# A graph-transformer kernel: attention folded in ahead of the last feed-forward's output, experts ranked by logits, and the expert tiles' rows, tables and transposes rearranged

## The chip, the cores and the metric

The kernel runs on one core of one Trainium2 chip. Five engines work in parallel, each with its own in-order queue: PE (TensorE, matrix products and transposes; PEld is its weight load), DVE (VectorE), ACT (ScalarE), POOL (GpSimd) and SP (SyncE). SP issues most transfers and holds a few registers; POOL issues the indirect gathers and scatters. They meet at semaphores. The metric is the device time of one execution in microseconds (us); lower is better.

## The reference, cut to what matters

A node table `x` of 3125 rows by 256 goes through two layers. The first adds, to the input, graph attention over 50,000 edges and a four-layer mixer (linear attention and a feed-forward each); then a mixture of eight experts, two for each node, adds its output. The second layer has another aggregation, another mixer and a dense mixture; nothing of it changes here.

```python
xn = _layernorm(x, axis=-1)
x = x + _L0_gnn_ref(xn, edge_index, ...) + _L0_mix_ref(xn[None], ...)[0]
x = x + _L0_ffn_ref(_layernorm(x, axis=-1)[None], ...)[0]
...
def _L0_ffn_ref(x, gate_w, gate_b, W1, b1, W2, b2):
    logits = xf @ gate_w + gate_b
    probs = jax.nn.softmax(logits, axis=-1)
    top2_vals, top2_idx = jax.lax.top_k(probs, 2)
    cw = jnp.zeros((N, Ee)).at[jnp.arange(N)[:, None], top2_idx].add(top2_vals)
    def step(acc, params):
        w1, bb1, w2, bb2, we = params
        h = jax.nn.gelu(xf @ w1 + bb1, approximate=False)
        y = h @ w2 + bb2
        return (acc + we[:, None] * y, None)
```

All of it is in 32-bit floats. The kernel computes for each node only the two experts with the largest weights, which is the same sum.

## The kernel before, in words

The 3125 nodes are 25 tiles of 128 rows (`NT`; the last has 53). `X`, with all of them, stays in SBUF from start to end.

**The first layer** is one Python loop over the generator `mixer()`. Each `yield` is a turn. In a turn the loop may also take steps of `edges()` (the graph attention, `todo`) and of the first generator in the list `late`. Such side work is put under `queued()` (L303), which says that it is to be issued after the last instruction so far of DVE, ACT and PE; the builder then fixes one order for each engine, and it may place an instruction among those of its neighbours. SP and POOL are not bound by `queued()`.

In the last mixer layer the feed-forward runs over the groups of `LATE`: first three tiles (22 to 24), then five groups of four, then two tiles. The text here calls the last two of these groups 5 and 6. For each group eight products with `w1` (L280 `mm`, hidden features `f`), each followed by a Gelu on ACT (L688), fill `gT`; then for each tile of the group a product with `w2` (L280 `acc`) is added to `X` by DVE (L699). Each product is a turn and each tile is a turn. After a group, `late.append(dispatch(t0, n))` (L706) hands it to the side work.

**`dispatch`** does, for the tiles of one group:
- loads the input rows `x0` (L250) and the attention's sums `ac` (L772), and adds both to `X` with the scale of the running maximum (L775 to L789);
- takes a layer norm (L260 to L264, with a square root on ACT) and normalises the rows into `hd` (L268);
- transposes `hd` on PE (L274), copies on ACT to `hx` (L802), and multiplies by the gate weights (`seg<-wt,hx`): logits `lg` (L806);
- softmax (L316 to L323, an Exp on ACT), rank of each expert among the eight probabilities (L812 to L821, `over`, `took`), weights `cw` (L823);
- transposes `cw` (L329), multiplies by the experts' output biases (L335) and adds to `X` (L336);
- counts on PE how many earlier rows took each expert (L831, L832), from which DVE forms the row `slot` of each token in its expert's stretch of the table `tok` (L836 to L846), and the weights `gate` (L848 to L850);
- POOL writes each row of `hd` to `tok` twice (L854, one indirect transfer per tile and choice).

After the loop whatever is left in `late` is run to its end. Then DVE builds tables (L881 to L932): how many 256-row tiles each expert needs, and for each of the `MT` = 32 tiles its expert `exI`, its first row in `tok` `rowI`, and its biases `b1`; and `slot` is corrected for the padding between experts.

**The expert tiles** (L943 on). For each of 32 tiles SP reads `exI` and `rowI` into registers, and loads two weight blocks (512 KB each) and the 256 rows `hr` (256 KB); three buffers each. PE transposes the rows (L956), DVE copies them to `hTe` (L958), PE makes four products of 128 hidden features (`mm<-hTe,ew`), each with a Gelu on ACT (L963), then the two output products (`acc<-ew,egT`); DVE copies the result to `yo` (L968) and ACT's queue stores it to `yex` (L969). From tile 8 on, every third tile also loads one expert of the second layer's weights (L973). After the loop the second layer gathers from `yex` by `slot`.

The memory of the expert stage's pool is memory that the first layer's pools have released, and the release counts all uses of those pools.

Of the kernel before, what the change touches and what calls it, by code (L numbers as in the profile page):

```python
# [8 lines left out]
F32 = mybir.dt.float32  # L9
# [10 lines left out]
L = 4  # L20
# [167 lines left out]
def fast_path(ctx: ExitStack, tc: tile.TileContext, i, out, ident, dstP):  # L188
# [171 lines left out]
    with ExitStack() as l0:  # L360
# [169 lines left out]
        def mixer():  # L530
# [5 lines left out]
            for l in range(L):  # L536
# [144 lines left out]
                for c, (t0, n) in enumerate(chunks):  # L681
                    nxt = chunks[c + 1][1] if c + 1 < len(chunks) else 0
                    gT = big.tile([Q, NF, n * Q], F32, name="gT", tag="kv", bufs=2)
                    for f in range(NF):
                        pm = ps("mm", [Q, n * Q])
                        product(pm, [w1[:, k, f * 128:(f + 1) * 128] for k in range(KC)],
                                [hT[:, k, t0:t0 + n, :].rearrange("p j c -> p (j c)") for k in range(KC)])
                        nc.scalar.activation(gT[:, f, :], pm, AF.Gelu, bias=col("b1", l * NF + f))  # L688
                        if f % 2 and f // 2 < nxt:
                            ff.rows(c + 1, f // 2)  # L690
                        yield 0.45 * n / NT / NF
# [72 lines left out]
        def dispatch(t0, n):  # L764
# [26 lines left out]

            mv, rs = ln_stats(xs, n)
# [12 lines left out]
            pr = g0.tile([Q, 4, NE], F32, name="lg", tag="lg", bufs=2)[:, 0:n, :]  # L805
            nc.vector.tensor_tensor(pr, pg, bc(gb, 1, n), ALU.add)  # L806
            softmax_of(g0, pr)
            yield
# [3 lines left out]
            nc.vector.tensor_tensor(over, bc(pr, 2, NE), bc(pr, 3, NE), ALU.is_equal)  # L812
            of = over.rearrange("p t e f -> p t (e f)")
            nc.vector.tensor_tensor(of, of, bc(below.rearrange("p e f -> p (e f)"), 1, n), ALU.mult)
            nc.vector.tensor_tensor(more, bc(pr, 2, NE), bc(pr, 3, NE), ALU.is_gt)
            nc.vector.tensor_tensor(over, over, more, ALU.add)
            def small(name):
                return g0.tile([Q, 4, NE], F32, name=name, tag=name, bufs=2)[:, 0:n, :]
# [3 lines left out]
            cw = small("cw")  # L822
            nc.vector.tensor_tensor(cw, took, pr, ALU.mult)  # L823
            yield
            yield from add_biases(g0, t0, n, cw, bt, tag="gt", bufs=3)
# [21 lines left out]
            for k in range(2):  # L847
                nc.vector.tensor_tensor(sel, at, bc(sf[:, k, :], 2, NE), ALU.is_equal)  # L848
                nc.vector.tensor_tensor(sel, sel, cw, ALU.mult)
                nc.vector.tensor_reduce(gate[:, k, t0:t0 + n], sel, AX.X, ALU.add)  # L850
            for j in range(n):
                r = rows(t0 + j)
                for k in range(2):
# [4 lines left out]
                    tc.declare_no_dep(put.ins, group="tok", reason="no two tokens have the same row of an expert")  # L858

# [4 lines left out]
        for step in mixer():  # L864
# [4 lines left out]
            if late:  # L869
                with queued():  # L870
                    if next(late[0], 0) == 0:
                        late.pop(0)
# [6 lines left out]


        tiles = g0.tile([Q, NE], F32, name="tiles", tag="tiles")  # L881
        nc.vector.tensor_tensor(tiles, used, first, ALU.subtract)
        nc.vector.tensor_scalar(tiles, tiles, float(ME - 1), None, op0=ALU.add)
        ti = g0.tile([Q, NE], I32, name="ti", tag="ti")
        nc.vector.tensor_copy(ti, tiles)
        nc.vector.tensor_scalar(ti, ti, 8, None, op0=ALU.logical_shift_right)
        nc.vector.tensor_copy(tiles, ti)
        upto = g0.tile([Q, NE], F32, name="upto", tag="upto")
        nc.vector.tensor_copy(upto, tiles)
        for e in range(1, NE):  # L890
            nc.vector.tensor_tensor(upto[:, e:e + 1], upto[:, e - 1:e], upto[:, e:e + 1], ALU.add)
        nth = g0.tile([Q, MT], F32, name="nth", tag="nth")
        nc.gpsimd.iota(nth, pattern=[[1, MT]], base=0, channel_multiplier=0, allow_small_or_imprecise_dtypes=True)
        eoh = g0.tile([Q, MT, NE], F32, name="eoh", tag="gt", bufs=3)
        nc.vector.tensor_tensor(eoh, bc(upto, 1, MT), bc(nth, 2, NE), ALU.is_le)
        ex = g0.tile([Q, MT], F32, name="ex", tag="ex")
        nc.vector.tensor_reduce(ex, eoh, AX.X, ALU.add)
        nc.vector.tensor_scalar(ex, ex, float(NE - 1), None, op0=ALU.min)
        exI = const.tile([Q, MT], I32, name="exI", tag="exI")
        nc.vector.tensor_copy(exI, ex)  # L900
        eidx = g0.tile([Q, NE], F32, name="eidx", tag="eidx")
        nc.gpsimd.iota(eidx, pattern=[[1, NE]], base=0, channel_multiplier=0, allow_small_or_imprecise_dtypes=True)
        nc.vector.tensor_tensor(eoh, bc(eidx, 1, MT), bc(ex, 2, NE), ALU.is_equal)

        nc.vector.tensor_tensor(tiles, upto, tiles, ALU.subtract)
        nc.vector.scalar_tensor_tensor(tiles, tiles, -float(ME), first, op0=ALU.mult, op1=ALU.add)
        pick = g0.tile([Q, MT, NE], F32, name="pick", tag="gt", bufs=3)
        nc.vector.tensor_tensor(pick, eoh, bc(tiles, 1, MT), ALU.mult)
        row = g0.tile([Q, MT], F32, name="row", tag="row")
        nc.vector.tensor_reduce(row, pick, AX.X, ALU.add)  # L910
        nc.vector.scalar_tensor_tensor(row, nth, float(ME), row, op0=ALU.mult, op1=ALU.add)
        nc.vector.tensor_scalar(row, row, float(NE * ST - ME), None, op0=ALU.min)
        rowI = const.tile([Q, MT], I32, name="rowI", tag="rowI")
        nc.vector.tensor_copy(rowI, row)
        b1 = const.tile([Q, MT, HB], F32, name="b1", tag="b1")
        be = cols_of("e_b1").rearrange("p (e f) -> p f e", f=HB)
        for f in range(HB):
            nc.vector.tensor_tensor(pick, eoh, bc(be[:, f, :], 1, MT), ALU.mult)
            nc.vector.tensor_reduce(b1[:, :, f], pick, AX.X, ALU.add)


        step = g0.tile([Q, NE], F32, name="step", tag="step")
        nc.vector.tensor_copy(step, tiles)
        nc.vector.tensor_tensor(step[:, 1:NE], tiles[:, 1:NE], tiles[:, 0:NE - 1], ALU.subtract)
        sp = g0.tile([Q, 2 * NT, NE], F32, name="sp", tag="gt", bufs=3)
        sl = slotF.rearrange("p k t -> p (k t)")
        nc.vector.tensor_tensor(sp, bc(sl, 2, NE), bc(first, 1, 2 * NT), ALU.is_ge)
        nc.vector.tensor_tensor(sp, sp, bc(step, 1, 2 * NT), ALU.mult)
        back = g0.tile([Q, 2 * NT], F32, name="back", tag="back")
        nc.vector.tensor_reduce(back, sp, AX.X, ALU.add)  # L930
        nc.vector.tensor_tensor(back, sl, back, ALU.subtract)
        nc.vector.tensor_copy(slot.rearrange("p k t -> p (k t)"), back)  # L932

# [6 lines left out]
    with ExitStack() as l0e:  # L940
# [3 lines left out]
        for k in range(MT):  # L944
            re = nc.values_load(exI[0:1, k:k + 1], engines=(SPE,), min_val=0, max_val=NE - 1)
            rr = nc.values_load(rowI[0:1, k:k + 1], engines=(SPE,), min_val=0, max_val=NE * ST - ME)
            w1 = ew.tile([Q, KC, EH], F32, name="ew1", tag="ew1", bufs=3)
            nc.sync.dma_start(w1, i["e_W1"][bass.ds(re, 1), :, :].rearrange("o (k p) c -> p (o k) c", p=Q))
# [1044 lines left out]
```

## Time and profile before

| what | us |
|---|---|
| median of 3 runs (2812.88 to 2814.0) | 2813.36 |
| the profiled execution | 2967.99 |
| its span | 2966.2 |
| PE busy (89% of the span) | 2640.8 |
| DVE busy (51%) | 1517.6 |
| ACT busy (29%) | 873.5 |
| POOL busy (31%) | 917.0 |
| share of the chain that ended last on PE | 79% |

The profile is one execution under the hardware profiler, which is longer than the runs without it. Its page gives busy times, the span in slices, the chain of work that ended last, and groups of instructions. The trace behind it answers questions about a stretch, an engine or a tile: a line of a timeline has the start, the duration, engine, line of the kernel, operation, output and inputs, shape and count, and in brackets the idle time before it with what ended it. A matrix product of 32-bit floats appears as two PE instructions, so `x16` is eight products. In the tile names, numbers of buffers are left out: `ew` is either weight block of an expert, `w` either block of the feed-forward. The mean granted PE clock of the profiled execution is 0.945 of full speed.

### The profile page before, as it was taken

The numbers are of one execution on the slowest core, as the hardware profiler recorded it, in microseconds if no ns is written. First come the engines' busy times: TensorE is split into PE (matmuls) and PEld (weight loads), VectorE is DVE, ScalarE is ACT, GpSimd is POOL, SyncE is SP. The second block draws the span as 40 slices with busy tenths as digits, with TensorE's granted clock in tenths as the row PEclk, the third lists the DMA queues.
The fourth block names the chain that finished last, engine by engine and source line by source line (L and its number), as shares of the span: only waits on it lengthen the run. The fifth ranks groups of instructions, "written<-read, shape, count | busy, mean of one in ns | idle before, by whom it ended". The sixth has DMA issues, their size and how long they took to land.

```text
span 2966.2 us, 29959 instructions
## 1 busy us (share of the span) xinstructions
PE 2640.8 (89%) x10578; PEld 1891.9 (64%) x10578; DVE 1517.6 (51%) x3749; ACT 873.5 (29%) x1621; POOL 917.0 (31%) x964
## 2 busy tenths in 40 slices
PE   5899989989988779898998699856789999999998
PEld 4666768656676457686665588734556666666655
DVE  6376655856657557668556311176834333322211
ACT  3432225312252112343333122222233222322223
POOL 2107542144521335200122100065354544555200
PEclk9899999999999889999998799978889999999999
DMA  4002221022212121100111576442122222222100
GB/s 141 12 16 89 81 90 38 22 77 76 86 47 70 29 77 41 59 4 13 31 58 59 191 252 200 153 145 81 47 75 64 75 67 71 71 73 78 33 8 10
DMA packets 152337, 215.85 MB, mean 73 GB/s; under 512 B 21032, under 2 KB 120686, under 8 KB 152178
## 3 DMA queue, kind: packets, MB, share of 16 engines
q1 hardware_dynamic: 104274, 112.31, 11.7%
q0 software_dynamic: 36848, 91.34, 10.8%
q10 hardware_dynamic: 11056, 10.19, 1.1%
q8 instruction: 86, 1.41, 0.2%
q14 instruction: 73, 0.60, 0.1%
HBM read 160.14 MB, written 53.61 MB: 72 GB/s over the span
## 4 chain that ended last, share of the span: by engine, by line
PE 79%; DVE 10%; another core or an unknown queue 4%; issue 3%; ACT 2%; DMA 1%; POOL 0%; SPq 0%; DVEq 0%; ACTq 0%
PE mm L280 33%; PE acc L280 24%; PE seg L467 6%; PE seg L1241 6%; PE acc L614 3%; PE tr L274 3%; PE seg L280 1%; PE acc L335 1%; DVE vals L457 1%; DVE gt L422 1%; DVE st L521 1%; DMA raw<-in_src 0%; PE tr L280 0%; DVE hT L737 0%
## 5 line engine op out<-in xcount | busy, mean ns | idle before, releaser
L283 POOL DMA_INDIRECT gt<-table,srcI x391 | 426.9, 1092 | 807.1 <-DVE m L425 602.9
L283 POOL DMA_INDIRECT gt<-xtab,srcI x391 | 381.7, 976 | 394.8 <-PE seg L1241 241.9
L280 PE MATMUL mm<-hT,w 128*128 128x512 f32 (+2 forms) x896 | 381.7, 562 | 23.7 <-ACT gT L688 16.2
L280 PE MATMUL acc<-w,gT 128*128 128x256 f32 x1600 | 370.0, 387 | 6.2 <-issue 4.2
L280 PEld LDWEIGHTS acc<-w,gT 128*128 128x128 f32 x1600 | 306.4, 194 | 53.1 <-issue 6.9
L1182 ACT ACTIVATE fh<-mm,bn_b,bn_s 128x512 f32<-128x512 f32 (+1 forms) x224 | 163.1, 731 | 425.8 <-PE mm L280 391.9
L280 PEld LDWEIGHTS mm<-hT,w 128*128 128x128 f32 x896 | 164.5, 193 | 158.8 <-issue 100.0
L339 DVE SCALAR_TENSOR_TENSOR X<-acc,rw,X 128x256 f32<-128x256 f32 x200 | 95.1, 483 | 325.9 <-PE acc L280 277.2
L688 ACT ACTIVATE gT<-mm,cols 128x512 f32<-128x512 f32 (+2 forms) x224 | 142.3, 641 | 354.0 <-PE mm L280 263.5
L280 PE MATMUL mm<-wqkv,hT 128*128 128x256 f32 x800 | 214.2, 399 | 15.6 <-ACT hT L723 9.0
L467 PE MATMUL seg<-vals,oh 128*128 128x261 f32 x782 | 192.0, 399 | 13.3 <-DVE oh L290 8.7
L280 PE MATMUL acc<-fw_f_Wo,fh 128*128 128x256 f32 x800 | 198.4, 385 | 1.6 <-issue 0.7
L280 PE MATMUL mm<-fh,fw_f_W 128*128 128x512 f32 (+1 forms) x448 | 195.3, 565 | 1.6 <-ACT fh L1182 1.3
L1241 PE MATMUL seg<-gt,oh 128*128 128x256 f32 x782 | 186.6, 388 | 3.8 <-DVE sum L1258 2.7
L280 PE MATMUL mm<-xc,fw_f_W 128*128 128x512 f32 (+1 forms) x448 | 188.9, 551 | 0.0
L467 PEld LDWEIGHTS seg<-vals,oh 128*128 128x128 f32 x782 | 152.9, 198 | 52.8 <-DVE oh L290 15.7
L280 PEld LDWEIGHTS acc<-fw_f_Wo,fh 128*128 128x128 f32 x800 | 144.7, 190 | 59.1 <-issue 27.9
L1241 PEld LDWEIGHTS seg<-gt,oh 128*128 128x128 f32 x782 | 150.4, 194 | 38.5 <-issue 12.8
L280 PEld LDWEIGHTS mm<-wqkv,hT 128*128 128x128 f32 x800 | 144.2, 197 | 40.4 <-ACT K L566 11.4
L699 DVE TENSOR_TENSOR X<-acc,X 128x256 f32<-128x256 f32 x100 | 42.2, 422 | 220.8 <-PE acc L280 149.2
L1020 POOL DMA_INDIRECT ye<-yex,slot x50 | 51.5, 1030 | 297.4 <-DVE cb L1087 273.8
L280 PEld LDWEIGHTS mm<-fh,fw_f_W 128*128 128x128 f32 x448 | 78.2, 191 | 99.5 <-issue 68.7
(329 smaller groups left out, 3877.0 us busy)
## 6 DMA issues: line engine op xcount, KB each, us to landing
ew<-in_e_W SPq DMA_DIRECT2D x64, 512.0 KB
tok<-zero SPq DMA_DIRECT2D x8, 3328.0 KB
w<-in_W SPq DMA_DIRECT2D x8, 1024.0 KB
hr<-tok SPq DMA_DIRECT2D x32, 256.0 KB
yex<-yo ACTq DMA_DIRECT2D x32, 256.0 KB
gt<-table,srcI POOLq DMA_INDIRECT x391
gt<-xtab,srcI POOLq DMA_INDIRECT x391
fw_f_W<-in_f_W SPq DMA_DIRECT2D x16, 256.0 KB
```

The lines of the kernel that those rows point to most:

```text
L274: nc.tensor.transpose(pt[:, k, :], src_row[:, k * Q:(k + 1) * Q], ident)
L280: nc.tensor.matmul(pm, a, b, start=(k == 0), stop=(k == len(lhs) - 1))
L283: nc.gpsimd.indirect_dma_start(out=dst, out_offset=None, in_=tab[:, :], in_offset=bass.IndirectOffsetOnAxis(ap=srcI[:, b:b + 1], axis=0))
L335: nc.tensor.matmul(py, cT[:, j, :], bt, start=True, stop=True)
L339: nc.vector.scalar_tensor_tensor(X[:, t, :], py, cw, X[:, t, :], op0=ALU.mult, op1=ALU.add)
L467: nc.tensor.matmul(open_seg[w_], oh[:, b - h0, :], v[:, b - h0, :], start=(b == a), stop=(b == z))
L614: nc.tensor.matmul(cx[a], K[0:r, t, a * 128:(a + 1) * 128], keys.hn[0:r, t, :], start=(t == 0), stop=(t == NT - 1))
L688: nc.scalar.activation(gT[:, f, :], pm, AF.Gelu, bias=col("b1", l * NF + f))
L699: nc.vector.tensor_tensor(X[:, t, :], py, X[:, t, :], ALU.add)
L1020: nc.gpsimd.indirect_dma_start(out=ye[0:r, j, :], out_offset=None, in_=yex[:, :], in_offset=bass.IndirectOffsetOnAxis(ap=slot[0:r, k, t0 + ...
L1182: nc.scalar.activation(hn[:, a, 0:w], pm, AF.Relu, bias=bn[s][1][:, c:c + 1], scale=bn[s][0][:, c:c + 1])
L1241: nc.tensor.matmul(segs[w], oh[:, j, :], gt[:, j, :], start=(b == z), stop=(b == a))
```

## The change

`dispatch` is cut in two. Its first part, the attention and the input rows, becomes `fold`, which is put at the head of `late` at the start of each group of the last feed-forward, so that it is added to `X` before the group's output is. While more than one generator waits in `late`, two steps are taken in a turn.

In `dispatch` the rank is taken from the logits, before any softmax, which gives the same two experts. Counts, slots and the writes to `tok` follow at once; softmax, `cw`, the gate weights and the biases come after.

The first eight tiles of the expert stage are the first tile of each expert: their expert, row and bias are constants. `table_of_tiles` builds the tables for the other 24 (`MR`), in two parts that are taken after tiles 0 and 1; its correction of `slot` compares with two thresholds for each expert. A function `load` issues a tile's transfers, the rows ahead of the weights; three tiles are loaded ahead of the loop, and tile k+3 at the end of tile k. `turned` transposes a tile's rows, and tile k+1's are transposed in tile k, between its two products.

```diff
                     gT = big.tile([Q, NF, n * Q], F32, name="gT", tag="kv", bufs=2)
+                    if l == L - 1:
+                        late.insert(0, fold(t0, n))
...
-        def dispatch(t0, n):
+        def fold(t0, n):
...
             nc.vector.tensor_tensor(x4, x4, a4[:, :, :, 0:64], ALU.add)
             yield
 
+        def dispatch(t0, n):
+
+            xs = X[:, t0:t0 + n, :]
             mv, rs = ln_stats(xs, n)
...
-            nc.vector.tensor_tensor(pr, pg, bc(gb, 1, n), ALU.add)
-            softmax_of(g0, pr)
-            yield
+            lg = small("lg")
+            nc.vector.tensor_tensor(lg, pg, bc(gb, 1, n), ALU.add)
...
-            nc.vector.tensor_tensor(more, bc(pr, 2, NE), bc(pr, 3, NE), ALU.is_gt)
+            nc.vector.tensor_tensor(more, bc(lg, 2, NE), bc(lg, 3, NE), ALU.is_gt)
...
-            cw = small("cw")
-            nc.vector.tensor_tensor(cw, took, pr, ALU.mult)
             yield
-            yield from add_biases(g0, t0, n, cw, bt, tag="gt", bufs=3)
...
-            for k in range(2):
-                nc.vector.tensor_tensor(sel, at, bc(sf[:, k, :], 2, NE), ALU.is_equal)
-                nc.vector.tensor_tensor(sel, sel, cw, ALU.mult)
-                nc.vector.tensor_reduce(gate[:, k, t0:t0 + n], sel, AX.X, ALU.add)
             for j in range(n):
                 r = rows(t0 + j)
                 for k in range(2):
...
+            yield
+
+            softmax_of(g0, lg)
+            cw = small("cw")
+            nc.vector.tensor_tensor(cw, took, lg, ALU.mult)
+            for k in range(2):
+                nc.vector.tensor_tensor(sel, at, bc(sf[:, k, :], 2, NE), ALU.is_equal)
+                nc.vector.tensor_tensor(sel, sel, cw, ALU.mult)
+                nc.vector.tensor_reduce(gate[:, k, t0:t0 + n], sel, AX.X, ALU.add)
+            yield
+            yield from add_biases(g0, t0, n, cw, bt, tag="gt", bufs=3)
...
             if late:
-                with queued():
-                    if next(late[0], 0) == 0:
-                        late.pop(0)
+                for _ in range(2 if len(late) > 1 else 1):
+                    with queued():
+                        if late and next(late[0], 0) == 0:
+                            late.pop(0)
...
-        for k in range(MT):
-            re = nc.values_load(exI[0:1, k:k + 1], engines=(SPE,), min_val=0, max_val=NE - 1)
-            rr = nc.values_load(rowI[0:1, k:k + 1], engines=(SPE,), min_val=0, max_val=NE * ST - ME)
...
+        def load(k):
+            if k < NE:
+                v1, v2, rr = i["e_W1"][k:k + 1, :, :], i["e_W2"][k:k + 1, :, :], k * ST
+                src = tok[rr:rr + ME, :]
+            else:
+                re = nc.values_load(exI[0:1, k - NE:k - NE + 1], engines=(SPE,), min_val=0, max_val=NE - 1)
+                rr = nc.values_load(rowI[0:1, k - NE:k - NE + 1], engines=(SPE,), min_val=0, max_val=NE * ST - ME)
...
+            hr = ew.tile([Q, 2, D], F32, name="hr", tag="hr", bufs=3)
+            nc.sync.dma_start(hr, src.rearrange("(j p) c -> p j c", p=Q))
             w1 = ew.tile([Q, KC, EH], F32, name="ew1", tag="ew1", bufs=3)
...
+        loaded = {k: load(k) for k in range(3)}
+        hT = turned(loaded[0][2])
+        table = table_of_tiles()
+        for k in range(MT):
+            w1, w2, _ = loaded.pop(k)
...
+            if k + 1 < MT:
+                hT = turned(loaded[k + 1][2])
             py = ps("acc", [Q, 2, D])
...
             nc.scalar.dma_start(yex[k * ME:(k + 1) * ME, :].rearrange("(j p) c -> p j c", p=Q), yo)
+            next(table, None)
+            if k + 3 < MT:
+                loaded[k + 3] = load(k + 3)
```

The new `table_of_tiles` has some 45 DVE operations, as many as the block that it replaces; its last part is

```diff
+            sp = tmp("sp", [2 * NT, 2 * NE])
+            sl = slotF.rearrange("p k t -> p (k t)")
+            nc.vector.tensor_tensor(sp, bc(sl, 2, 2 * NE), bc(thr.rearrange("p e s -> p (e s)"), 1, 2 * NT), ALU.is_ge)
+            nc.vector.tensor_tensor(sp, sp, bc(inc, 1, 2 * NT), ALU.mult)
+            back = tmp("back", [2 * NT])
+            nc.vector.tensor_reduce(back, sp, AX.X, ALU.add)
```

## The prediction

> **What bounds the kernel now.** I read the chain of waits first, then busy time by stretch, then the waits inside one stretch. TensorE (PE) carries 79% of the chain that ended last, so only stretches where PE idles or runs slowed are worth anything. The change touches two stretches: from the last mixer layer's feed-forward to the first expert tile, and the 32 expert tiles. The view of busy time by stretch (us in the stretch, busy PE, PEld, DVE, ACT, POOL; clock; DMA share; GB/s):
>
> ```profile
> 1500.00:1550.00 50.00, 48.91 (x214) 35.63 (x213) 26.83 (x100) 14.94 (x22) 14.25 (x15) 1.00 0.19 64
> 1550.00:1600.00 50.00, 46.76 (x206) 32.23 (x205) 25.09 (x95) 22.34 (x34) 8.47 (x8) 1.00 0.17 54
> 1600.00:1620.00 20.00, 14.36 (x60) 11.69 (x58) 12.62 (x53) 3.79 (x8) 4.88 (x6) 0.79 0.12 40
> 1620.00:1650.00 30.00, 12.57 (x38) 7.99 (x38) 22.18 (x107) 3.33 (x6) 14.88 (x15) 0.50 0.22 75
> 1650.00:1665.00 15.00, 0.67 (x4) 0.70 (x4) 5.52 (x16) 0.00 (x0) 0.35 (x1) 0.50 0.43 144
> 1700.00:1800.00 100.00, 94.96 (x454) 81.16 (x455) 16.12 (x26) 24.66 (x52) 0.00 (x0) 1.00 0.74 241
> ```
>
> The feed-forward is PE-bound (48.9 and 46.8 of 50 us busy). Then PE nearly stops for some 55 us. In the tile loop it is busy for 95 of 100 us. The PE timeline and the chain give the gap's ends:
>
> ```profile
> 1600.86 8.86 PE L280 MATMUL acc<-w,gT 128*128 128x256 f32 x32
> 1613.72 0.82 PE L274 MATMUL tr<-ident,hd 128*128 128x128 f32 x4 [4.00 <-DVE gate L850]
> 1634.32 1.09 PE L274 MATMUL tr<-ident,hd 128*128 128x128 f32 x4 [4.91 <-DVE hd L268]
> 1664.33 1.08 PE L956 MATMUL tr<-ident,hr 128*128 128x128 f32 x4 [18.79 <-DMA hr<-tok]
> ...
> 1658.93 4.73 DMA hr<-tok
> 1663.67 0.66 issue
> 1664.33 1.10 PE tr L956 x4
> 1665.45 0.70 DVE hTe L958
> 1666.20 3.70 PE mm L280 x8
> ```
>
> The last output row ends at 1600.86+8.86 = 1609.72; the first expert product starts at 1666.20: 56.5 us. [...] The stations between: slots of group 4 and group 5's normalised rows to 1613.72 (4.0); its gate products to 1618.59 (4.9); its softmax and ranks to 1622.46 (3.9); its counts, slots and biases, with group 6's attention, to 1632.02 (9.6); group 6 from statistics to slots to 1645.51 (13.5); writes, tile tables and SP's register reads to the first load at 1657.74 (12.2); loads, transposes and copy to 1666.20 (8.5). Inside the loop the waits between 1680 and 1920 us (total, times, longest) are:
>
> ```profile
> PEld mm L280 <- DVE hTe L958: 16.0, 15, 1.1
> PE mm L280 <- DVE hTe L958: 12.4, 15, 0.8
> PEld mm L280 <- ACT egT L963: 3.2, 16, 0.4
> ```
>
> Every second tile PE stands about 1.07 us until the transposed rows are copied.
>
> **Transposes a tile ahead.** The built instruction order puts tile k+1's four transposes among tile k's up-products and its copy (0.69 us) beside the down-product (3.46 us). A pair of tiles takes 15.82 us (1684.30 to 1700.12), of which the stall is 1.07 and the rest work that stays. Sixteen pairs: 17 us less, about 7.38 us a tile. What is late next? The loads: the stretch 1700 to 1750 us moves 275 GB/s at share 0.85; the faster pace asks 275x7.91/7.38 = 295 GB/s, share 0.91. Rows of 10 us reach 302 GB/s at 0.88, and 353 in the first burst, and loads have two tiles (15 us) of lead. I count no loss; the upper bound is the whole 17 us. Moving each row load ahead of its weights helps the transposes; a row load and two weight loads cost SP three issues of 0.37 us as before.
>
> **Tile tables and registers.** Before, the tables (DVE, 1643.73 to 1655.66) and 13 reads of 0.42 us on SP (to 1657.74) stand ahead of the first load. After, the first eight tiles have constant rows; 48 reads remain of 64 and fall in the loop, where SP waits for buffers anyway. The tables' some 45 small DVE operations (10 us, and 1.5 more for the slot correction of doubled width) lie beside the first row load and tile 0. If that cover failed, tile 1's copy would be late: some 14 of them (5 us) stand between the copies of tiles 0 and 1, and tile 0 takes 9. Cost nothing.
>
> **But the loads cannot start early.** In the built order SP's first row load waits, because its buffers reuse released memory, for all row writes, the last Exp, the last bias product and the last gate reduction; the weights queue behind it. So softmax, gates and biases are moved behind the writes in the text, yet are still waited for. They fit in DVE's gaps while POOL, which has nothing else here, writes; they cost no more than their places in the queues.
>
> **The drain, counted from the last row's end.** DVE (one addition, the logits of group 5, 13 more operations at the start-to-start intervals seen at 1620, 0.1 to 0.45 us) has group 6's normalised rows ready at 4.5. PE holds ahead of them group 5's counts (1.05) and the transposes of its weights `cw` (1.04), which need the softmax: DVE reaches `cw` at 7.2, so group 6's transposes start at 8.4. With the gate products and four bias products between them they end at 13.0 (alone, before, 1634.32 to 1637.38). Ranks to 16.0, counts 1.05, slots (2.7 us before, plus two bias additions) to 20.7. POOL: group 5's eight writes start at 10.0 and take 8x1.27 = 10.2, up to 11 us; the four of group 6 follow from 20.9 to 26.0. Landing: no row shows it alone; a 256 KB store lands in 2.13, a gather in 6.16; I take 2.1 as a write is nearer a store: 28.1, and SP issues at 28.4. The row load is now first: between 2.13 and the 4.73 seen with 1 MB ahead; I take 2.9, then 1.10 and 0.75 for transposes and copy: 33.2. The first weights (0.77 MB at 353 GB/s and 2.1) land about then. **33.3 us in place of 56.5: 23 saved**; bounds 12 (slow landings, DVE 4 us later) and 28.
>
> Here the Trainium skill speaks against the change: its page "ScalarE: Activation LUTs", section "What ACT_TABLE_LOAD costs", prices each change of table at 2.66 us, load and drain. The Exp table now stands between group 6's square root and group 5's weights. The row:
>
> ```profile
> 1592.11 1.28 ACT L318 ACT_TABLE_LOAD   x1
> 1593.40 0.23 ACT L318 ACTIVATE lg<-lg 128x32 f32<-128x32 f32 x1
> ```
>
> Exp starts 0.01 us after a load of 1.28, with no drain. By the row Exp is done at 4.4, well ahead of DVE's turn; by the page at 5.8, which costs `cw` at most 0.3. The number of loads does not change. I take the row. The Trainium skill's page "TensorE: Matmul & The Clock Gate", Part 1 on the HAM clock gate, has the clock halved until about 3.4 us of sustained work. One might hope that the shorter drain spares the cold start. The first eight PE instructions of expert products take 3.70 us, later eights 1.73: 2.0 us. The idle left (33 us) is still far over that window, so by rule and row those 2.0 us stay, and drain products keep the slow rows' price; a hope of 2 us more is dropped.
>
> **Attention ahead of the output.** `fold` is the same work, moved ahead by one group: DVE's six operations of up to 1.23 us and two loads a group. Both loads pass to before the group's products on SP's queue; SP does nothing else there but edge-table stores, which still come first for the first group. The built order has each load's buffers free long before use; in the first group the table (issued 1400.32) is needed near 1404, a wait DVE can afford as PE has three output rows of 3.46 us queued. Two steps a turn crowd DVE (25 to 27 of 50 us busy) no further on average, but one 1.22 us addition ahead of an evacuation can hold PE. Bounds: 4 us gained (all idle of 1500 to 1600) to 8.5 lost (1.22 for each of 7 groups); I take 2 lost, as idle now is under a microsecond per place. Group 5's gate products now stand ahead of the last row's final products: 2 us of work and as much waiting for copies less overlap, 3 us (0 to 5).
>
> **Sum.** -17 -23 +2 +3 = -35 us on the profiled execution of 2967.99 us (span 2966.2 and 1.8 around it). The median of the runs is 2813.36, 0.948 of it; I scale: -33. **2780 us.** Everything before the last layer's feed-forward and after the loop keeps its order.
>
> **Rivals.**
> - *Loads bind the loop* (15%). For: share 0.9 in several rows at 10 us, and the last experts' weights share the queue. Against: 0.6 after 1760. The loop gains 5: -23, so 2791.
> - *The drain hardly shortens* (13%), since the first load waits for everything: only tables, registers and load order go: the last write ends at 1650.35, with landing 1652.8 instead of 1657.74, and 3.6 on the load: -8.6. With the loop -25: 2789. Against: group 6's attention (over 3 us) and its softmax leave that chain for certain.
> - *Drain overlaps better* (8%), no harm to the feed-forward: -45, 2771.
> - *Slower* (4%). DVE stands in its queue for a fold's table load, with X additions and hT behind it, so PE stops. Price: a wait beyond 3.46 us of cover for each of seven groups; from 5 us exposed per group it decides, at 6 it is 42 lost: 2820. For: the fold computes one turn after its loads, not two. Against: buffers are free early in the built order, and DVE had no such wait at 1602.
> - The likeliest, as summed: 60%.
>
> **Range and chances.** The likeliest's own bounds, combined, give 2768 to 2793; the second and first rival reach 2791, the fourth 2771; to leave out no more than 2 in 10 I take 2766 to 2798. The three runs lie within 0.04%, and 0.2% (5.6 us) is about what a measurement of this kernel can tell from no change: faster by more 0.93, within 0.03 (a small stall of the slower kind), slower 0.04.
>
> **What would show it.** Waits of PE on the copied rows gone and about 7.4 us a tile; no register reads ahead of the first load; some 33 us between last output row and first expert product, with POOL's writes ending about 26 after it; PE idle between 1400 and 1600 about as now. Wrong if PE waits for DVE on rows of the fold, if tiles wait for weights, or if the gap stays over 45 us.

## The result, and the profile after

The changed kernel takes 2773.47 us (median of four runs, 2770.17 to 2777.46) where the kernel before takes 2813.45 (four runs, 2812.88 to 2814.0): a ratio of 0.9864, 95% interval 0.9847 to 0.9881, 40 us less. The forecast was 2780, 33 less. The profiled execution of the changed kernel took 2773.55 us (span 2771.8), as its runs do; so it is not the profiler that made the first profile of before longer than its runs.

The first profile of the kernel before, on which the forecast was built, spans 2966.2 us, 194 more than that of the changed kernel. Most of this is not the change, so a second profile of the kernel before was taken; it spans 2805.8. The table cuts each profile at the same instructions: the start of the last linear-attention product (`acc<-hn,K`), the first product of the last layer's feed-forward, the end of its last output product, the first expert product, the end of the last down-product, the first transpose of `xn` behind the loop, and the end of the span. All stages are differences of start times that the trace gives; where a stage ends with a product, its 0.38 us is added.

| us | before, first profile | before, second | after |
|---|---|---|---|
| start to the last linear-attention product | 1319.9 | 1209.8 | 1209.9 |
| to the feed-forward | 70.8 | 69.6 | 69.6 |
| last feed-forward | 218.9 | 218.9 | 221.3 |
| drain (last output row to first expert product) | 56.5 | 57.1 | 34.6 |
| 32 expert tiles | 254.3 | 254.3 | 238.2 |
| loop's end to `xn` | 21.9 | 21.9 | 21.9 |
| from there to the end | 1023.9 | 974.2 | 976.3 |

Between the two profiles of before, 160 us of difference lie in the first and the last row, and almost nothing in the stages that the change touches. Against the second profile the change brings 2.4 - 22.5 - 16.1 = -36.2 us in its three stages, and the spans differ by 34.0.

Busy time by stretch of the changed kernel (us in the stretch, busy PE, PEld, DVE, ACT, POOL; granted clock; DMA share; GB/s): the end of the feed-forward, cut where PE falls idle and where the clock changes, the drain, and 200 us of the tile loop.

```profile
1481.33:1483.38 2.05, 0.00 (x0) 0.00 (x0) 0.72 (x4) 2.02 (x3) 1.45 (x2) 1.00 0.31 110
1483.38:1493.62 10.24, 9.30 (x23) 6.18 (x24) 5.08 (x19) 2.49 (x4) 4.29 (x5) 0.50 0.19 68
1493.62:1500.86 7.24, 7.24 (x46) 6.17 (x44) 2.33 (x8) 1.29 (x4) 0.00 (x0) 1.00 0.01 2
...
1500.00:1520.00 20.00, 12.20 (x42) 8.08 (x41) 11.48 (x60) 2.77 (x6) 7.78 (x8) 0.60 0.13 48
1520.00:1535.00 15.00, 3.26 (x9) 1.87 (x8) 7.15 (x38) 0.00 (x0) 3.84 (x4) 0.50 0.38 122
```

```profile
1550.00:1750.00 200.00, 200.00 (x981) 174.83 (x980) 37.96 (x55) 51.40 (x109) 0.00 (x0) 1.00 0.77 247
```

In the loop PE is now busy for all of 200 us at full clock: no wait is left there to remove. The drain has shrunk but still has PE idle and at half clock. And inside the feed-forward PE falls idle at 1481.33, and from 1483.38 on the clock is at half for 10.24 us. The kernel before has a stall of another form at the same place; it is taken up below.

PE's timeline of the changed kernel across the drain (start, us, operation, count, and in brackets the idle time before it and what ended it):

```profile
1499.75 1.11 PE L280 MATMUL acc<-w,gT 128*128 128x256 f32 x4
1500.69 0.51 PE L280 MATMUL seg<-wt,hx 128*128 128x8 f32 x4
1504.29 0.64 PE L831 MATMUL seg<-took,earlier 128*128 128x32 f32 x2 [3.09 <-DVE took L824]
...
1507.66 0.64 PE L274 MATMUL tr<-ident,hd 128*128 128x128 f32 x2
...
1514.58 1.22 PE L335 MATMUL acc<-bt,cwT 8*128 8x256 f32 x2
1518.15 0.60 PE L831 MATMUL seg<-took,earlier 128*128 128x16 f32 x2 [2.35 <-DVE sm_r L322]
...
1533.63 1.08 PE L982 MATMUL tr<-ident,hr 128*128 128x128 f32 x4 [10.95 <-DVE upto L917]
1535.50 3.78 PE L280 MATMUL mm<-hTe,ew 128*128 128x256 f32 x8 [0.78 <-DVE hTe L984]
```

The last output row ends at 1500.86 and the first expert product starts at 1535.50. Group 5's gate products (`seg<-wt,hx`) now stand among the last row's products. Group 6's transposes start 6.8 us after the row. The last wait is put down to DVE's `upto`, which these transposes do not read. It is the row load that ends it: when the rows are issued behind the weights (below), the same transposes start 4.3 us later, and in the kernel with both edits (below) the view names `hr<-tok` itself.

### The profile page after: what moved, and what is told of

It is laid out like the page before. It is cut to its first block, busy times and chain, and to the rows that moved or that the text cites. A ratio compares the mean times of both kernels' runs of the same rounds, so it can differ in the third digit from the quotient of the medians.

```text
span 2771.8 us, 29883 instructions
## 1 busy us (share of the span) xinstructions
PE 2596.2 (94%) x10578; PEld 1875.5 (68%) x10578; DVE 1523.5 (55%) x3754; ACT 870.6 (31%) x1619; POOL 932.1 (34%) x962
## 4 chain that ended last, share of the span: by engine, by line
PE 83%; DVE 10%; ACT 2%; DMA 2%; issue 2%; POOL 1%; SPq 0%; DVEq 0%; ACTq 0%; POOLq 0%
PE mm L280 35%; PE acc L280 26%; PE seg L467 6%; PE seg L1280 6%; PE acc L614 3%; PE tr L274 3%; PE acc L335 1%; POOL gt L283 1%; PE seg L280 1%; DVE gt L422 1%; DVE kv L1116 1%; DMA ye<-yex,slot 1%; PE tr L280 1%; PE tr L982 1%; DVE kv L1118 0%
## 5 line engine op out<-in xcount | busy, mean ns | idle before, releaser
L283 POOL DMA_INDIRECT gt<-table,srcI x391 | 439.3, 1124 | 690.3 <-DVE m L425 496.5
L280 PE MATMUL mm<-hT,w 128*128 128x512 f32 (+2 forms) x896 | 372.6, 555 | 10.1 <-ACT gT L690 8.6
L467 PE MATMUL seg<-vals,oh 128*128 128x261 f32 x782 | 184.0, 387 | 3.7 <-DVE vals L457 3.7
L1280 PEld LDWEIGHTS seg<-gt,oh 128*128 128x128 f32 x782 | 149.5, 193 | 33.3 <-issue 13.0
```

Source lines behind the costliest of these rows:

```text
L280: nc.tensor.matmul(pm, a, b, start=(k == 0), stop=(k == len(lhs) - 1))
L283: nc.gpsimd.indirect_dma_start(out=dst, out_offset=None, in_=tab[:, :], in_offset=bass.IndirectOffsetOnAxis(ap=srcI[:, b:b + 1], axis=0))
L467: nc.tensor.matmul(open_seg[w_], oh[:, b - h0, :], v[:, b - h0, :], start=(b == a), stop=(b == z))
L1280: nc.tensor.matmul(segs[w], oh[:, j, :], gt[:, j, :], start=(b == z), stop=(b == a))
```

## The experiments

For each, the stages are read from its profile as in the table above; "the two" are feed-forward and drain together (276.0 in the second profile of before, 255.9 after). Times of whole runs scatter by 3 to 7 us either way around a median, so where a few us matter the stages decide, and runs are compared with the kernel before on the same chip. Each stage is read from one profile, and a feed-forward carries a chance of its own: its first products follow the same two waits (1.07 and 1.18 us) in every profile, yet in three of the fourteen (transposes left out, attention put back, all tiles from the tables) the clock falls to half just behind them. The first line is the changed kernel's, the second that of transposes left out:

```profile
1279.54 2.85 PE L280 MATMUL mm<-hT,w 128*128 128x384 f32 x8 [1.18 <-DVE hT L739]
1280.84 4.54 PE L280 MATMUL mm<-hT,w 128*128 128x384 f32 x8 [1.18 <-DVE hT L739]
```

No edit of these kernels touches what stands ahead of these products, so the 1.7 us are taken off those three feed-forwards where they are compared below.

### The kernel before, profiled again

No edit.

> The kernel before, unchanged, for a second profile. Its first profile spans 2966.2 us, 153 more than its runs; the profile after spans what its runs take. Theory A (mine, in the form of the forecast's scaling): the excess lies evenly over the span, so the drain (last output row's end to first expert product) would be 56.5 x 0.948 = 53.6 us and a pair of tiles 15.0 us in an ordinary execution. Rival B: the excess lies in single stalls elsewhere, and both stretches are as the first profile shows: drain 56 to 57 us, pairs of tiles 15.8 us, last feed-forward 219 us. A span near 2812 us would make the two profiles comparable stage by stage.

The run took 2807.54 us, its span is 2805.8. Theory A fell: drain 57.1 and loop 254.3 are those of the first profile. The excess lies outside. In the first profile some 4% of the chain are waits for "another core or an unknown queue", of which the second has none:

```profile
PE 79%; DVE 10%; another core or an unknown queue 4%; issue 3%; ACT 2%; DMA 1%; POOL 0%; SPq 0%; DVEq 0%; ACTq 0%
```

```profile
PE 81%; DVE 11%; ACT 2%; DMA 2%; issue 2%; POOL 1%; SPq 0%; DVEq 0%; ACTq 0%; POOLq 0%
```

The first line is from the first profile's page, part 4, the second from the second's. A saving read in these stages was therefore to be taken at its full size.

### Transposes ahead, alone and left out

Alone, in the kernel before (tables, order of loads and the rest as they were):

```diff
+        loaded = {k: load(k) for k in range(3)}
+        hT = turned(loaded[0][2])
         for k in range(MT):
+            w1, w2, _ = loaded.pop(k)
...
+            if k + 1 < MT:
+                hT = turned(loaded[k + 1][2])
             py = ps("acc", [Q, 2, D])
```

> The kernel before with the transposes a tile ahead alone (all tiles still read their rows and experts from the tables, the weights are still issued ahead of the rows). My theory: the stall of 1.07 us in each of 16 pairs goes and nothing else changes: 16 to 17 us less than before, about 2797 us, 7.35 to 7.4 us a tile. Rival (the loads bind, or the stall only moves): 0 to 8 us less. Rival (the transposes are worth more because the whole loop was slowed by it): over 20 us less.

Left out of the changed kernel:

```diff
-            w1, w2, _ = loaded.pop(k)
+            w1, w2, hr = loaded.pop(k)
+            if k:
+                hT = turned(hr)
...
-            if k + 1 < MT:
-                hT = turned(loaded[k + 1][2])
```

> The changed kernel with each tile's rows transposed in the tile itself, as before; all else of the change stays. My theory: the stall returns, 16 to 17 us more than the changed kernel, about 2790 us, 23 less than before; 7.9 us a tile. If the loads with fixed rows or the new load order took part in the loop's gain, the stall returns only in part: under 12 us more.

Alone: 2795.1 us, ratio 0.9941 (0.9924 to 0.9958), 16.5 us less than before on that chip; loop 237.4, all other stages as before. Left out: 2791.21 us, ratio 0.9924 (0.9907 to 0.9940); loop 255.2, 17.0 more than in the changed kernel, drain 34.6 as there; feed-forward 223.0, or 221.3 without the 1.7, as there. The loop's gain is the transposes' and nothing else's. Waits on the copied rows in the loop, second profile of before (total us, times, longest); the changed kernel has no PE wait at all between 1550 and 1760 us:

```profile
PEld mm L280 <- DVE hTe L958: 15.0, 14, 1.1
PE mm L280 <- DVE hTe L958: 11.7, 14, 0.8
```

### The attention put back behind the output

```diff
-                    if l == L - 1:
-                        late.insert(0, fold(t0, n))
...
         def dispatch(t0, n):
+            yield from fold(t0, n)
```

> The changed kernel with the attention of each group put back behind its output rows, at the head of the ranking; the two steps a turn, the logits, the fixed rows and the transposes ahead stay. My theory: the chain of the last group again holds its attention (3 to 4 us on DVE, its loads done long before), and the queue of the group before it is longer; the drain becomes 6 to 10 us longer and the feed-forward gains back the 2 us counted for the fold's place: 4 to 8 us more than the changed kernel. Rival: the fold ahead is worth most of the drain's gain: 12 to 20 us more. Rival: it is worth nothing or harms: 0 to 4 us less.

2772.67 us, ratio 0.9860 (0.9839 to 0.9881): no difference in time from the changed kernel. The stages show a trade: feed-forward 217.2, drain 41.0 (6.4 more). Without the 1.7 the feed-forward is 215.5, 5.8 less, and the two are 256.5, 0.6 more than in the changed kernel. The drain moved as my theory said, the feed-forward by three times what it said, so the 4 to 8 us forecast for the two did not come. About 2 of the 5.8 are work that changes sides (23 PE instructions, group 5's transposes and gate products; by the estimate given under the softmax below). The rest is less waiting and less time at half clock: 3.41 us near the end of the feed-forward here, 10.24 in the changed kernel.

### One step of side work a turn

```diff
-                for _ in range(2 if len(late) > 1 else 1):
+                for _ in range(1):
```

> The changed kernel with one step of the side work a turn instead of up to two, the attention still ahead of the output. My theory: a group has 12 turns and now some 15 steps, so the ranking falls behind by about three steps a group and two groups or so are left for the drain: the drain grows by 10 to 25 us, the feed-forward shrinks by 5 to 10 (less side work in it): 5 to 15 us more than the changed kernel. Rival: the second step is not needed and only crowds DVE: 0 to 4 us less.

2781.52 us, ratio 0.9899 (0.9875 to 0.9924). Feed-forward 203.8 (17.5 less), drain 64.7 (30.1 more): the two 12.6 more, within the forecast, though each part is larger than forecast. The last output row ends near 1483.5. Behind it PE's timeline shows the counts of two groups of four tiles (32 columns) ahead of the last group's, where the changed kernel has one:

```profile
1498.23 0.64 PE L831 MATMUL seg<-took,earlier 128*128 128x32 f32 x2 [3.01 <-DVE took L824]
...
1515.15 0.64 PE L831 MATMUL seg<-took,earlier 128*128 128x32 f32 x2 [2.58 <-DVE took L824]
...
1527.60 0.61 PE L831 MATMUL seg<-took,earlier 128*128 128x16 f32 x2 [2.24 <-DVE took L824]
```

The second step a turn is what keeps the queue of side work short, and the largest single part of the drain's gain.

### Softmax and biases ahead of the counts

```diff
+            softmax_of(g0, lg)
+            yield
...
+            nc.vector.tensor_tensor(cw, took, lg, ALU.mult)
             yield
+            yield from add_biases(g0, t0, n, cw, bt, tag="gt", bufs=3)
...
-            softmax_of(g0, lg)
-            cw = small("cw")
-            nc.vector.tensor_tensor(cw, took, lg, ALU.mult)
```

> The changed kernel with the softmax, the weights and the biases put back ahead of the counts, so that the ranks compare probabilities; all else stays. My theory: the last group's chain holds its softmax again (about 1 us of DVE, an Exp, and its table load) and both groups' biases stand ahead of the slots: drain 4 to 8 us longer, the same number more in all. Rival (the first load waits for the softmax and the biases anyway, so their place does not matter): within 2 us of the changed kernel.

2767.56 us, ratio 0.9852 (0.9833 to 0.9872): faster than the changed kernel, if anything. The drain has the length that my theory gave (41.9, 7.3 more), though hardly for its reason, as a later kernel shows; to the feed-forward the theory was blind: 210.5, 10.8 less; the two 252.4, 3.5 less. Of the 10.8 about 2.6 are work that moved into the drain: 21 PE instructions. (An estimate: PE is busy for 217.4 us in the changed kernel's feed-forward and 210.1 here, and half of the 9.30 us that it is busy at half clock is counted as lost.) The rest is the stall of the changed kernel. ACT's timeline there, and PE's below it:

```profile
1480.51 0.47 ACT L690 ACTIVATE gT<-mm,cols 128x256 f32<-128x256 f32 x1 [0.39 <-PE mm L280]
1481.00 1.28 ACT L318 ACT_TABLE_LOAD   x1
1482.29 0.23 ACT L318 ACTIVATE lg<-lg 128x32 f32<-128x32 f32 x1
```

```profile
1483.55 1.01 PE L329 MATMUL tr<-ident,cw 128*8 128x128 f32 x4 [2.22 <-DVE cw L859]
1485.33 3.80 PE L335 MATMUL acc<-bt,cwT 8*128 8x256 f32 x8 [0.77 <-DVE cwT L331]
1489.06 7.68 PE L280 MATMUL acc<-w,gT 128*128 128x256 f32 x24
```

Group 4's softmax comes late: its input is ready at 1480.81, the table load starts behind the seventh of the eight Gelus of group 6's features, and the weights `cw` follow at 1483.40. PE has finished those features' products at 1481.33 and holds the transposes of the weights next, so it stands for 2.22 us, and 0.77 more for the copy. Then the clock is down: the eight bias instructions take 3.80 us (four took 1.12 at full clock, so 2.24 for eight: 1.6 lost), the next 24 output instructions 7.68 (16 take 3.62 at full clock, 24 some 5.4: 2.3 lost). Three us of waiting cost some seven. With softmax first the same transposes wait 0.38 us and the clock stays at 1.00.

The change did not bring this stall, though. The kernel before has softmax first and stalls at the same place: the Exp and two table loads stand ahead of a Gelu of group 6's features, and PE waits for that Gelu. From its first profile (the second has the same waits):

```profile
1595.47 1.13 PE L280 MATMUL mm<-hT,w 128*128 128x256 f32 x4 [1.72 <-ACT gT L688]
1598.44 2.34 PE L335 MATMUL acc<-bt,cwT 8*128 8x256 f32 x8 [0.77 <-DVE cwT L331]
```

Over the whole feed-forward PE waits 4.4 us before and has the clock at half for 6.8; in the changed kernel 4.0 and 10.2; with softmax first 0.4 and none. So the rest of the change removes the stall of before, and the late softmax puts another in its place. Softmax, weights and biases moved together in this kernel; which of them matters most was not separated.

### All tiles from the tables; rows behind weights

The first: `load(k)` reads expert and row of every tile from tables built ahead of the loop. The second:

```diff
-            hr = ew.tile([Q, 2, D], F32, name="hr", tag="hr", bufs=3)
-            nc.sync.dma_start(hr, src.rearrange("(j p) c -> p j c", p=Q))
             w1 = ew.tile([Q, KC, EH], F32, name="ew1", tag="ew1", bufs=3)
...
+            hr = ew.tile([Q, 2, D], F32, name="hr", tag="hr", bufs=3)
+            nc.sync.dma_start(hr, src.rearrange("(j p) c -> p j c", p=Q))
             return w1, w2, hr
```

> The changed kernel with all 32 tiles taken from the tables, built ahead of the loop as before, with SP's register reads; attention ahead, logits and transposes ahead stay. My theory: the tables can start with the last counts, so they stand partly beside the writes; what is left in sight is the last table operations and SP's reads of 0.42 us: drain 4 to 6 us longer. Rival: the tables stand wholly behind the last write as in the changed kernel (its table operations waited for the last row write): 12 us or more longer. Rival: under 2 us, nothing in sight.

> The changed kernel with each tile's weights issued ahead of its rows, as before. My theory: the first rows land behind 1 MB of weights, 1 to 2 us later, and the loop keeps its 7.35 us a tile: 1 to 2 us more. Rival: the weights are needed at the same time anyway: within 0.5 us in the drain. Rival: the transposes of the next tile come late in each tile: 5 us more or over.

Tables: 2774.96 us, ratio 0.9880 (0.9861 to 0.9900); drain 40.9, 6.3 more, just over the range I gave; the feed-forward is 223.0, or 221.3 without the 1.7, as in the changed kernel. The tables did start beside the writes, at 1521.92, so the first rival fell. The last row write starts at 1528.54 and SP's first load at 1536.70, 8.2 later; in the changed kernel 1527.29 and 1529.93, 2.6 later.

Rows last: 2774.85 us, ratio 0.9881 (0.9861 to 0.9900); feed-forward 221.4, drain 39.0, 4.3 more, over twice what I expected, and no harm in the loop (237.8). SP issues its first load at 1529.91 as in the changed kernel, but the rows are third:

```profile
1530.84 0.50 SPq L975 DMA_DIRECT2D hr<-tok  x1
```

```profile
1537.93 1.09 PE L982 MATMUL tr<-ident,hr 128*128 128x128 f32 x4 [15.27 <-DMA ew<-in_e_W]
```

From issue to first transpose 7.1 us with 1 MB ahead; in the changed kernel, with rows first, 3.7 (1529.93 to 1533.63).

### Looking for a better order

The stall of the feed-forward and the bias products between group 5 and group 6 suggested three kernels: group 5's softmax, weights and biases behind group 6's writes (`weigh_last`); softmax first only for the groups ranked within the feed-forward (`softmax_first_in_ff`); and both.

```diff
+            soon = t0 not in (LATE[-2][0], LATE[-1][0])
+            if soon:
+                softmax_of(g0, lg)
+                yield
...
+            if t0 == LATE[-2][0]:
+                rest.append(weigh(t0, n, soon, lg, cw, took, at, sf, sel))
+            else:
+                yield from weigh(t0, n, soon, lg, cw, took, at, sf, sel)
```

> The changed kernel with group 5's softmax, weights, gates and biases put behind group 6's row writes; the groups before keep the changed kernel's order. In the trace of the changed kernel group 6's four transposes start 6.9 us after the last output row's end and its gate products end 7 us later, because group 5's weights and bias products stand between them. Theory: without these in between they end about 5 us earlier, and POOL becomes the bound (eight writes of group 5 at 1.26 us, then four): drain 4 to 5 us shorter, feed-forward unchanged. Rival (the first load waits for the biases, which now come last): within 1 us or longer.

> The changed kernel with softmax, weights and biases ahead of the counts in the groups that are ranked within the feed-forward, and the changed kernel's order in groups 5 and 6. In the changed kernel group 4's Exp comes behind the last Gelu of group 6's features and its table load; PE waits 2.2 us for the weights, and the granted clock is 0.5 to 0.64 for the 10 us that follow. Theory: this wait and its slow clock go: feed-forward 6 to 8 us shorter, drain as in the changed kernel (34 to 36 us): 6 to 8 us less. Rival (the shorter feed-forward of the kernel with softmax first was only work pushed into the drain): feed-forward at most 3 us shorter, or the drain longer by as much as is gained.

> Both edits at once: softmax and biases ahead of the counts within the feed-forward, group 5's behind group 6's writes. Theory: the two gains add, 10 to 13 us less than the changed kernel, some 2760 us. Rival: they share the same idle time, and one of them is lost: 5 to 8 us less.

These three ran on a chip where the kernel before takes 2969.0 us: 2929.16, 2936.16 and 2929.28, ratios 0.9872 (0.9841 to 0.9904), 0.9874 (0.9841 to 0.9908) and 0.9875 (0.9853 to 0.9896). The changed kernel did not run there, so in time they say little. Stages: `weigh_last` has drain 31.5, 3.1 less, short of the 4 to 5 forecast (feed-forward 223.6: the stall is there, and one more stretch of 3.41 us at half clock). POOL writes twelve times without a pause in it, as expected, and is its bound. The other two have feed-forward 216.5 and drains of 41.0 and 38.6, so the two are 257.4 and 255.2: neither forecast came, and for `softmax_first_in_ff` its rival did, the drain longer by as much as is gained. That kernel also shows that the softmax's place in the last groups is hardly what lengthens the drain of softmax first: it has the changed kernel's order in groups 5 and 6, and its drain is still 41.0, 0.9 shorter. In both, group 5's transposes and gate products have fallen behind the last output row; why their turn comes later there is open. In `softmax_first_in_ff` and in the kernel with both edits PE has five waits in the feed-forward (4.8 us together in the former) where the instruction order on PE and ACT is that of softmax first, which had none, so the kernel with both edits ran once more:

> The kernel of e9_both once more. Its first profile came from a chip on which the kernel before takes 2969 us and on which the engines stood for a queue that the profile cannot name; five waits in its feed-forward (4.8 us together) have no releaser in the built order. Theory: on a chip like the first ones the feed-forward takes 210 to 212 us, as with softmax first, and the drain 35 to 38: the two together 246 to 250 in place of 255.9, and 6 to 10 us less than the changed kernel (ratio to before some 0.983). Rival: the waits belong to the order, feed-forward 216 and drain 38 to 39 again, no gain over the changed kernel.

2764.21 us (2763.21 to 2766.22), ratio 0.9841 (0.9821 to 0.9862). Feed-forward 210.6, drain 38.7, the two 249.3, 6.6 less than the changed kernel: theory held for the sum, with the drain 0.7 over its range. The five waits are gone, so they do not belong to the order; what makes them is open, as `weigh_last` has none of them on the same chip. This kernel has the lowest ratio of the study, though its interval overlaps those of softmax first and of the changed kernel; the stages are what separates them. The gains did not add to the 10 to 13 us first expected, and the 5 to 8 of that rival came: the drain is 4 us longer than with the changed order, because group 5's gate products fall behind the last row again. The drain still ends in twelve writes in a row, which start every 1.27 us from 1507.42 to 1521.34.

## Why the prediction was right, point by point

- **Transposes a tile ahead, -17.** Measured -16.9 alone and -16.1 within the change (254.3 to 237.4 and 238.2). A tile takes 7.35 us (1549.90 to 1557.25 between two groups of down-products); 7.38 was forecast. Loads did not bind: 276 GB/s at share 0.87 in the first 50 of these 200 us and 247 at 0.77 over all, not 295 at 0.91.
- **Drain, -23.** Measured -22.5. Counted from the last row, forecast and found: group 6's rows ready 4.5 and 3.7; its transposes start 8.4 and 6.8; ranks 16.0 and 17.2; slots 20.7 and 22.3; group 5's writes start 10.0 and 8.6; the last write ends 26.0 and 27.4; first load 28.4 and 29.1; first product 33.3 and 34.6. The number owes something to luck: from the start of group 6's transposes to its ranks, with the gate and bias products between, 7.6 us were forecast and 10.4 found, and an earlier start took 1.6 of these 2.8 back. The row load took 3.7 in place of 2.9. The write was seen to land 2.4 us after its start, so after its end it takes only 1.4, not 2.1.
- **What the drain's gain consists of** was not split in the forecast. Undone one at a time, feed-forward and drain together, with the 1.7 us taken off where they apply: two steps a turn 12.6, fixed first tiles 6.3, rows ahead of weights 4.4, attention ahead 0.6, logits and late softmax -3.5. The sum, 20.4, is near the measured 20.1. Each part is one profile, so 0.6 is nothing that can be told from none, but the -3.5 is borne out by the stall: one part works against the rest.
- **Attention ahead +2, gate products +3.** Measured together +2.4. By the same estimate as above 1.6 of it is work (group 5's transposes and gate products, 23 PE instructions), 1.3 more time lost at half clock, and 0.4 less waiting. So +3 was too much, and the price of the fold cannot be read apart from the softmax's. Its ground, "idle now is under a microsecond per place", was misread: the first profile has the wait of 1.72 us at 1595.47.
- **"They cost no more than their places in the queues"**, said of the softmax and what follows it, is the step that failed. It was argued for the drain. Inside the feed-forward the new place lets PE come to the transposes of group 4's weights before their softmax is done; that costs some 7 us of wait and slow clock, which keeps the feed-forward about as stalled as before, and undoing it shortens feed-forward and drain together by 3.5. The term was counted as nothing. Of the rule weighed there (the Trainium skill, "ScalarE: Activation LUTs", section "What ACT_TABLE_LOAD costs": load and drain, 2.66 us) the row stayed right: 1.31 us from the seventh Gelu's end to the Exp, 1.28 of them the load, no drain. The mistake was not the price but where it was looked for.
- **The scaling by 0.948.** It assumed that the profiled execution was long everywhere. The second profile shows the three stages at the same length in an execution of 2807.54 us. Unscaled, -35 against stages of -36.2.
- **-33 forecast, -40 measured.** 2 us are the scaling. The profiled executions differ by 34.0 (2807.54 and 2773.55), so the rest is between executions: the stage from `xn` to the end, with the same code, ranges from 971.2 to 976.9 in the profiles without the unnamed queue. What part of the last 5 us is chance can't be told.
- **The rivals.** No load bound the loop, the drain did shorten, and no fold's load stopped DVE: PE has no wait for `x0` or `ac` rows in the feed-forward. The slower side did have a case, but another one: the late softmax. The sum of the second rival leaves out the +5 of the likeliest; with it the drain's failure would have meant some 2794.
- **Cold start.** The first eight expert products take 3.78 us, 3.70 before: that hope was rightly dropped.

## What to carry to other kernels

When work is moved, follow its first instruction on every in-order engine into every stage that it passes through, not only the stage for which it is moved: here a softmax that was moved for the drain stalls PE in the feed-forward, and undoing the move gives 3.5 us over both. And price a short stall of PE by what follows it as well as by its length. A sum made on a profile is checked against a second one, stage by stage, before it is scaled; and where a stage differs by 1 or 2 us, look first whether its clock started alike.

## What was not expected of the hardware

- **The clock falls after a shorter wait than the rule suggests.** The Trainium skill's "TensorE: Matmul & The Clock Gate", section "HAM oscillation — how this bites in real kernels", warns of idle gaps over about 3.4 us. Here the granted clock fell from 1.00 to 0.50 when PE had been idle for 2.05 us (1481.33 to 1483.38), and in all five profiles with this order it fell 2.0 to 3.4 us after PE had run dry there. With waits of 0.71, 1.36 and 0.21 us within 8 us (attention put back) it fell too.
- **It changes at times 3.41 us apart, which do not follow the program.** From the feed-forward's start to the end of the drain every stretch at half clock, in all fourteen profiles, lasts 3.41 us or a whole multiple (6.83, 10.24, and 30.7 to 64.9 over a drain), and the two falls in the changed kernel, at 1483.38 and 1503.86, are six times 3.41 apart. Counted on in steps of 3.413 us, the next such time behind the feed-forward's first product comes 0.9 us after it in the three profiles in which the clock fell there, and 2.1 to 2.5 us after it in the eleven in which it did not. So what a short wait costs seems to hang on where it lies between two such times. How busy PE must be in such a span is not shown here.
- **The same program takes 2801 to 2819 us on three chips and 2963 to 2977 on a fourth.** In profiles from there the engines wait for a queue without a name. The two profiles of one program (the kernel with both edits, spans of 2915.5 and 2762.1 us) differ by 95.7 us before the last linear-attention product and 52.7 behind the loop, and not in the expert tiles (237.4 and 238.4). The first profile of before has the same marks.
